# One-hot products in place of 16 gathers of the last pair but one, and the last sorts cut to 384 wide with a small write behind each operation

## The chip, the cores and the metric

The kernel runs on one core of a Trainium2 chip. The time is that of one execution of the program on the device, in microseconds (us). The engines are PE (matrix products), DVE (element-wise work on vectors), ACT (functions, scaled copies), POOL (here the issuer of all indirect transfers) and SP (the issuer of plain transfers). Each runs its own instructions in order; they wait for each other by semaphores.

## What is computed

The input is a batch of 16 graphs of 1024 nodes with 64 channels each, and an adjacency matrix of 1024 x 1024 per graph. Features are normalized, some neighbours of each node are dropped, and then each node takes, channel by channel, three quantiles of its remaining neighbours:

```python
h = jnp.maximum(_layernorm(x, axis=-1), 0.0)
...
rem = neigh & (sk > 1) & (rank % sk == sk - 1) & mask[:, :, None]
rem = rem | jnp.swapaxes(rem, 1, 2)
nd = jnp.where(rem, 0.0, adj_) > 0
s = jnp.sort(jnp.where(nd[..., None], x[:, None, :, :], jnp.inf), axis=2)
...
for tau, w in zip((0.25, 0.5, 0.75), (0.25, 0.5, 0.25)):
    agg = agg + w * (v_lo + frac * (v_hi - v_lo))
out = x + agg
y = jnp.maximum(out @ W1 + b1, 0) @ W2 + b2
```

Here `x` is the normalized `h`; the layer's result is the input plus `y`. `v_lo` and `v_hi` are the sorted neighbours at the two ranks around `tau` times the count of neighbours less one.

## The kernel before

**Stages.** The graphs go in pairs, 0 to 7. For each graph, `prepare` loads the adjacency, drops edges, orders the nodes by their count of neighbours, and writes a list of neighbour indices (`collect`, which leaves `lists[b]`). The normalized features go to a table in device memory (`gtab`). Then every node's neighbours are gathered from that table, sorted channel by channel by a network of minima and maxima, weighted, summed on PE, put back in the nodes' own order by a product with a one-hot matrix (`one_hot`, tile `at_p`, and `sums`), and sent through the two small dense layers (`mlp`).

**Tiles and classes.** After the ordering, a graph's nodes are 8 tiles of 128, the ones with most neighbours first. A tile's nodes have a fixed number of slots for neighbours; `FULL` says how many slots of each tile are gathered. `CLASSES` joins tiles with equal networks: tile 0 (13 slots), tiles 1 to 3 (11), tiles 4 and 5 (9), tiles 6 and 7 (7). The gathered values of a class and a pair lie in one tile of memory: `g0` and `g1` with two buffers, `g4` and `g6` with one, so the gathers of a pair for tiles 4 to 7 can't start before the sort of these tiles in the pair ahead is read. Nodes with very many neighbours (32 of each graph) get further slots in a sort of their own for every eight graphs, the group (`gg`, `aggregate_group`).

**Gathers.** One indirect transfer, issued by POOL, fetches one slot of one tile of one graph: 128 rows of 64 numbers (`gather` in `fetch`, L1332). A pair has 126 of them. The last pair has 70: for it the first slots of tiles 0 to 5 (`LEAST`: 8, 4, 4, 4, 4, 4, 0, 0 slots) are not gathered but computed by one-hot products, 56 in all.

**One-hot products.** `begin_pick` reads the features of the last pair's graphs back from the table (`xt`), splits each number into three parts of 16, 8 and 8 bits (`terms`) and turns the index lists to numbers (`index`). `pick` works through the wanted slots in chunks of eight: PE spreads each slot's indices over all partitions (`rowsT`, L1382), ACT copies them (`rows`, L1388), DVE compares them with the node numbers (`hot`, L1392, eight operations of 128x1024), PE multiplies (`got`, L1401, 8 products for each slot), ACT joins the parts in `g` (L1412, L1413). `hot` shares the tag "wide", of one buffer, with `rem` and `perm` of the preparation; `terms` shares "at", `index` shares "keys", both of two buffers; `xt` has one.

**Sorts.** `sort` goes through a plan of steps; a step is a minimum and a maximum over up to three pairs of slots at once (L1440, L1445, and L1437 where only one of them is wanted). Operations are at most `PART` = 384 elements wide, and each has a write of one column behind it (`opened`, the tile `pause`, L859). For the last pair and the last group (`whole`) they may be `WHOLE` = 1024 wide and have nothing behind them. From pair 5 on the weights are applied by ACT (L1460), for the group by DVE (L1462); then PE sums (L1466). In the last pair tiles 0 to 3 come first, then tiles 4 to 7 for one graph at a time.

**Order.** The loop over pairs at the end of `list_layer` only writes the program down: `weave` mixes the results of pair m - 1, the gathers and a side stream (preparation of later graphs, or `pick`). `arrange` then gives every engine an order of its own, for the whole program at once: it knows the dependences and a cost for each instruction (1345 ns for a gather), and goes forwards and backwards over the program six times with a list of ready instructions for each engine. It also ties each gather to instructions of DVE and ACT that its plan has 25 us earlier (`LEASH`). Buffers of one tag follow each other in the order in which the program names them. Small writes by `opened` follow their instruction directly.

Of the kernel before, what the change touches and what calls it, by code (L numbers as in the profile page):

```python
# [47 lines left out]
NT = N // P  # L48
# [16 lines left out]
CLASSES = (((0,), 13), ((1, 2, 3), 11), ((4, 5), 9), ((6, 7), 7))  # L65

LEAST = (8, 4, 4, 4, 4, 4, 0, 0)
# [3 lines left out]
GROUP = 8  # L71
# [481 lines left out]
ACTP, ACTB = 5, 13  # L553
# [259 lines left out]
def list_layer(  # L813
# [15 lines left out]
    B = x.shape[0]  # L829
# [463 lines left out]
    pairs = B // 2  # L1293
# [14 lines left out]
            turn[0] += 1  # L1308
            many = None if many is None else many - 1

    def opening(some, m=B // 2 - 1):

        tiles, slots = some
        if (m, tiles) not in gathered:
            gathered[m, tiles] = wk.tile(
                [P, PLANS[slots][0], len(tiles), 2, C], F32, name=f"g{tiles[0]}", bufs=2 - tiles[0] // 4
            )

    def fetch(m, classes=CLASSES, halves=(0, 1)):

        for tiles, slots in classes:
            lo, n = tiles[0], len(tiles)
            held, order = PLANS[slots][:2]

            def begin(h, tiles=tiles, lo=lo, n=n, slots=slots, held=held):
                opening((tiles, slots), m)
                nc.scalar.copy(gathered[m, tiles][:, slots - 1, :, h], owns[m][:, lo:lo + n, h])

            issued, given_out = paced

            def gather(h, slot, k, at, tiles=tiles, lo=lo):
                ins = nc.gpsimd.indirect_dma_start(  # L1332
                    out=gathered[m, tiles][:, slot, k - lo, h], out_offset=None, in_=tables[2 * m + h][0],
                    in_offset=bass.IndirectOffsetOnAxis(ap=lists[2 * m + h][:, at:at + 1], axis=0),
                    element_offset=tables[2 * m + h][1], engine_sem=issued,
                )
                given_out[ins.ins.name] = ins
                return ins

            for h in halves:  # L1340
                queue.append(partial(begin, h))
                for k in tiles:
                    for s, slot in enumerate(order[:FULL[k] + ((k, FULL[k]) in HOSTS)]):
                        if m < pairs - 1 or s >= LEAST[k]:
                            queue.append(partial(gather, h, slot, k, PASSED[k] + s))

    def begin_pick():

        first = wk.tile([P, NT], F32, name="first", bufs=1)
        nc.vector.tensor_tensor(first, own2.rearrange("p (t k) -> p t k", k=2)[:, :, 0], own2.rearrange("p (t k) -> p t k", k=2)[:, :, 1], OP.add)  # L1350
        nc.vector.tensor_scalar(first, first, float(FRONT), None, OP.add)
        terms, index = [], []
        for h in range(2):
            b = 2 * (pairs - 1) + h
            xt = wk.tile([P, NT, C], F32, name="xt", bufs=1)
            tab, at = tables[b]
            nc.sync.dma_start(
                out=xt, in_=tab[at // C + FRONT:at // C + FRONT + N].rearrange("(t p) c -> p t c", p=P)
            )
            t = wk.tile([P, NT, 3 * C], BF16, name="terms", tag="at", bufs=2)  # L1360
            halves, bytes_ = (
                xt.rearrange("p t c -> p (t c)").bitcast(d).rearrange("p (t c k) -> p t c k", t=NT, c=C)
                for d in (BF16, U8)
            )
            nc.scalar.copy(t[:, :, :C], halves[:, :, :, 1])
            nc.scalar.copy(t[:, :, C:].rearrange("p t (c k) -> p t c k", k=2), bytes_[:, :, :, 0:2])
            terms.append(t)
            f = wk.tile([P, PASSED[-1]], F32, name="index", tag="keys", bufs=2)
            nc.scalar.copy(f, lists[b])
            index.append(f)  # L1370
        return first, terms, index

    def pick(first, terms, index, wanted):

        m = pairs - 1
        for n in range(0, len(wanted), 8):
            some = wanted[n:n + 8]
            rows = wk.tile([P, len(some), P], F16, name="rows", tag="dist", bufs=2)
            for at in range(0, len(some), 4):
                tp = psum.tile([P, 4, P], F32, name="rowsT", tag="mx", bufs=3)  # L1380
                settle([
                    nc.tensor.matmul(  # L1382
                        tp[:, q], index[h][:, PASSED[k] + s:PASSED[k] + s + 1].to_broadcast([P, P]), ident32,
                        start=(q == 0), stop=(q == 3), skip_group_check=True,
                    )
                    for q, (h, k, s) in enumerate(some[at:at + 4])
                ])
                nc.scalar.copy(rows[:, at:at + 4], tp)  # L1388
            yield 0.5
            hot = wk.tile([P, NT, 8, P], BF16, name="hot", tag="wide", bufs=1)  # L1390
            for j in range(NT):
                opened(nc.vector.tensor_scalar(hot[:, j, :len(some)], rows, first[:, j:j + 1], None, OP.is_equal))  # L1392
                if j % 2:
                    yield 1.0
            for at in range(0, len(some), 2):
                (h, k, s), (h2, k2, s2) = some[at:at + 2]
                tiles, slots = next(c for c in CLASSES if k in c[0])
                to = PLANS[slots][1][s:s + 2]
                got = psum.tile([P, 2, 3 * C], F32, name="got", tag="code", bufs=2)
                settle([  # L1400
                    nc.tensor.matmul(  # L1401
                        got[:, q], hot[:, j, at + q], terms[h][:, j], start=(j == 0 and q == 0),
                        stop=(j == NT - 1 and q == 1), skip_group_check=True,
                    )
                    for q in range(2) for j in range(NT)
                ])
                opening((tiles, slots))
                step = to[1] - to[0]
                end = to[1] + (1 if step > 0 else -1)
                line = gathered[m, tiles][:, to[0]:end if end >= 0 else None:step, k - tiles[0], h]  # L1410
                halves, bytes_ = (line.bitcast(d).rearrange("p s (c k) -> p s c k", c=C) for d in (BF16, U8))
                nc.scalar.copy(halves[:, :, :, 1], got[:, :, :C])  # L1412
                nc.scalar.copy(bytes_[:, :, :, 0:2], got[:, :, C:].rearrange("p s (c k) -> p s c k", k=2))  # L1413
                yield 1.0
# [81 lines left out]
    def aggregate(m, o, between=None):  # L1496


        last = m == pairs - 1
        coef = coefs[m]  # L1500
        for half in (0, 1) if last else (1, 0):
            parts = CLASSES[2 * half:2 * half + 2][::1 if last else -1]
            for sides in ((0, 1), (1, 2)) if last and half else ((0, 2),):
                hs, one = slice(*sides), sides[0] if last and half else None
                if not one:
                    shape = [P, 4, 2, C] if one is None else [P, 2, 4, C]
                    tag, bufs = ("mx", 3) if last and not half else ("agg", 2)
                    whole = psum.tile(shape, F32, name="acc", tag=tag, bufs=bufs)
# [23 lines left out]
                for tiles, slots in parts:  # L1532
                    lo, n = tiles[0], len(tiles)
                    g = gathered[m, tiles]
                    plan = PLANS[slots]
                    if one is None:
                        lines, weigh = g.rearrange("p s n h c -> p s (n h c)"), partial(
                            lambda s, many, lo, n: coef[:, s:s + many, lo:lo + n].rearrange("p s n h -> p s (n h)"),
                            lo=lo, n=n,
                        )  # L1540
                    else:
                        lines, weigh = g[:, :, :, one], partial(
                            lambda s, many, lo, n, h: coef[:, s:s + many, lo:lo + n, h], lo=lo, n=n, h=one
                        )
                    yield from sort(
                        lines, plan, window(tiles, slots)[0], weigh, acc[:, lo - 4 * half:lo - 4 * half + n],
                        m >= ACTP, last,
                    )
                    if sides[1] == 2:
                        gathered.pop((m, tiles))  # L1550
# [143 lines left out]
    def aggregate_group(grp):  # L1694
# [9 lines left out]
        for k in range(n)[::-1]:  # L1704
            yield from sort(
                gg[:, :, k], PLANS[(CAP, SECOND + 1)[k]], window((0,), CAP)[0],
                lambda s, many: coef[:, s:s + many, k:k + 1], acc[:, k], whole=grp == B // GROUP - 1,
            )
        o = wk.tile([P, n * C], F32, name="go", tag="lows", bufs=1)
        nc.scalar.copy(o, acc.rearrange("p k c -> p (k c)"))  # L1710
# [79 lines left out]
    def drain(*gens):  # L1790
        for g in gens:
            for _ in g:
                pass
# [39 lines left out]
    for m in range(pairs + 1):  # L1833
# [15 lines left out]
            nc.vector.tensor_scalar(flag, fp, 0.0, None, OP.is_gt)  # L1849
        side = chain(*(prepare(b) for b in (2 * m + 2, 2 * m + 3) if b < B))  # L1850
        if m == pairs - 1:
            side = pick(*begin_pick(), [
                (h, k, s) for tiles, _ in CLASSES[:3] for h in range(2) for k in tiles for s in range(LEAST[k])
            ])
            for _ in range(20):
                next(side)
# [190 lines left out]
```

## Time and profile before

| | us |
|---|---|
| median of 3 runs | 1443.4 (1442.67 to 1445.76) |
| the profiled execution | 1448.98 |
| its span, first to last instruction | 1447.2 |
| busy: PE / DVE / ACT / POOL | 1100.0 / 1220.1 / 1041.4 / 1049.3 |
| DVE busy in 1350 to 1400 / 1400 to 1447 | 48.0 of 50 / 20.2 of 47 |
| gathers (L1332) from 1350 to 1400 | 27 |
| first and last hot operation (L1392) | 1155.7 and 1313.6 |

Times in the views are counted from the start of the span. A row of groups names the line, the engine, the operation and its tiles, then the count, the busy time in us and the mean ns of one, and behind the second bar the idle time of the engine just ahead of these instructions with what ended it. A row of the timeline has the start, the length, and in brackets the idle time ahead with its releaser. A row of the table by stage has the stage's limits, its length, and then the busy time and (x) the count for PE, PE's weight loads, DVE, ACT and POOL, the granted clock of PE as a share of full speed, the share of the transfer engines and GB/s. DVE's operations overlap a little: one starts before the record of the one ahead ends, so what an operation costs is the distance between starts.

### The profile page before, as it was taken

Reading aid. Unit: us, or ns where it says so; the run is one execution under the profiler, and the core shown is the slowest. Engines: PE = TensorE matmul, PEld = TensorE weight load, DVE = VectorE, ACT = ScalarE, POOL = GpSimd, SP = SyncE. Lnnn points to the kernel's source line nnn. Section 1 sums busy time; section 2 is a strip of 40 time slices with the busy share of each in tenths; the row PEclk is TensorE's granted clock in tenths of the full one; section 3 lists DMA queues with packets and bytes.
Section 4 is the critical chain, followed back from the end, with each engine's and each line's share of the span. In section 5 each row is a group of like instructions: output and inputs, shape, how many; then the busy total and the mean of one; then the engine's idle time right before and its main releaser. Section 6 shows DMA issues by size and latency. Waiting matters only on the chain. (4 is left out here: it accounts for less than half of the span.)

```text
span 1447.2 us, 30238 instructions
## 1 busy us (share of the span) xinstructions
PE 1100.0 (76%) x9011; PEld 706.0 (49%) x9011; DVE 1220.1 (84%) x5869; ACT 1041.4 (72%) x2869; POOL 1049.3 (73%) x991
## 2 busy tenths in 40 slices
PE   6877887999888985898479986599837995358167
PEld 4545555555555553555246554365514674125044
DVE  5646799978899899978799898998799779979765
ACT  8797698888959893879558773758839763449554
POOL 0277777777777777777777777777777777778880
PEclk9999998999999997899789997699969998669568
DMA  6453334333524252325332342422211111112110
GB/s 218 141 174 106 111 119 127 90 90 102 148 56 131 64 154 54 100 59 148 91 87 65 88 127 60 118 61 64 69 24 40 32 27 24 24 31 61 35 20 21
DMA packets 128831, 121.67 MB, mean 84 GB/s; under 512 B 95730, under 2 KB 96274, under 8 KB 128658
## 3 DMA queue, kind: packets, MB, share of 16 engines
q1 hardware_dynamic: 97106, 87.29, 19.9%
q0 software_dynamic: 31552, 32.36, 10.2%
q8 instruction: 73, 1.20, 0.3%
q14 instruction: 100, 0.82, 0.2%
HBM read 108.79 MB, written 9.05 MB: 81 GB/s over the span
## 5 line engine op out<-in xcount | busy, mean ns | idle before, releaser
L1332 POOL DMA_INDIRECT g<-gtab,idx x952 | 1013.1, 1064 | 354.3 <-DMA g<-gtab,idx 154.8
L1440 DVE TENSOR_TENSOR g<-g 128x384 f32<-128x384 f32 (+2 forms) x659 | 312.0, 494 | 25.3 <-DMA g<-gtab,idx 19.1
L1445 DVE TENSOR_TENSOR g<-g 128x384 f32<-128x384 f32 (+2 forms) x659 | 310.8, 493 | 5.5 <-DMA gg<-g 4.2
L1145 PE MATMUL codeP<-pack,perm 128*128 128x332 bf16 x1024 | 181.0, 318 | 54.3 <-DVE perm L1120 34.0
L1466 PE MATMUL acc<-g,kf 128*128 128x128 f32 (+2 forms) x472 | 137.6, 424 | 69.0 <-ACT g L1460 46.3
L1048 ACT ACTIVATE dist<-rk,bias 128x512 f16<-128x512 f32 x256 | 169.7, 723 | 23.8 <-DVE bias L1023 10.1
L1145 PEld LDWEIGHTS <-perm 128*128 128x128 bf16 x1024 | 94.1, 100 | 132.8 <-DVE perm L1120 48.2
L981 ACT ACTIVATE ne<-tp 128x512 fp8e4<-128x512 f32 x248 | 144.7, 640 | 12.5 <-PE tp L974 11.1
L1071 ACT ACTIVATE kept<-kp 128x512 fp8e4<-128x512 f32 x224 | 138.4, 642 | 14.3 <-PE kp L1066 5.8
L1460 ACT ACTIVATE g<-g,coef 128x64 f32<-128x64 f32 x336 | 89.2, 359 | 81.4 <-DVE g L1440 63.2
L968 PE MATMUL tp<-kb,sg 128*128 128x128 bf16 x1024 | 107.7, 232 | 47.9 <-ACT dist L1048 27.5
L961 ACT ACTIVATE sg<-at 128x1024 bf16<-128x1024 f32 x122 | 133.8, 1097 | 4.0 <-DMA at<-in_adj_dram 3.9
L1466 PEld LDWEIGHTS acc<-g,kf 128*128 128x128 f32 x472 | 81.5, 210 | 99.2 <-ACT g L1460 56.0
L1038 PE MATMUL rk<-kb,cnt 128*128 128x512 bf16 x256 | 102.2, 399 | 35.9 <-ACT dist L1048 24.1
L1043 PEld LDWEIGHTS <-ne 128*128 128x128 fp8e4 x1024 | 82.2, 101 | 86.0 <-issue 55.9
L859 DVE MEMSET pause<- 128x1 bf16 x2043 | 120.5, 59 | 0.0
L968 PEld LDWEIGHTS <-sg 128*128 128x128 bf16 x1024 | 79.9, 104 | 79.7 <-issue 57.5
L1043 PE MATMUL rk<-kw,ne 128*128 128x128 fp8e5 x1024 | 108.6, 227 | 0.0
L1158 ACT CAST st<-codeP 128x4 bf16<-128x4 f32 x128 | 21.4, 167 | 119.8 <-DVE rest L1156 88.2
L1066 PE MATMUL kp<-kw,rem 128*128 128x128 fp8e5 x1024 | 101.1, 219 | 0.0
L1061 PE MATMUL kp<-ne,kw 128*128 128x512 fp8e4 x256 | 97.5, 382 | 3.5 <-ACT dist L1048 1.4
L1062 PE MATMUL kp<-rem,kw 128*128 128x512 bf16 x256 | 97.5, 381 | 0.0
(202 smaller groups left out, 2371.6 us busy)
## 6 DMA issues: line engine op xcount, KB each, us to landing
at<-in_adj_dram SPq DMA_DIRECT2D x122, 512.0 KB
g<-gtab,idx POOLq DMA_INDIRECT x952
xt<-in_x_dram SPq DMA_DIRECT2D x16, 256.0 KB
y<-in_x_dram SPq DMA_DIRECT2D x16, 256.0 KB
gtab<-xt SPq DMA_DIRECT2D x16, 256.0 KB
out_dram<-y SPq DMA_DIRECT2D x14, 256.0 KB
spare<-in_adj_dram SPq DMA_DIRECT2D x6, 512.0 KB
gg<-g SPq DMA_DIRECT2D x32, 48.0 KB
```

Of the source, the lines that this page charges most:

```text
L859: tails[nc.vector.memset(pause[:, at:at + 1], 0.0).ins.name] = ins.ins.name
L961: nc.scalar.activation(sg, at, AF.Sign)
L968: run.append(nc.tensor.matmul(tp[:, s], sg[:, m * P:(m + 1) * P], ident16, start=(s == 0), stop=(s == 3 and t // 4 != n), skip_group_check ...
L981: nc.scalar.activation(to, tp, AF.Relu, saturate=False)
L1043: run.append(nc.tensor.matmul(rk[:, s * P:(s + 1) * P], ne[:, 4 * n + s, ts], upper, start=False, stop=(s == 3), skip_group_check=True,))
L1048: nc.scalar.activation(dist[:, n * HALF:(n + 1) * HALF], rk, AF.Abs, bias=bias[:, t:t + 1])
L1071: nc.scalar.activation(kept[:, 4 * n:4 * n + 4], kp, AF.Relu, saturate=False)
L1145: run.append(nc.tensor.matmul(flat, perm[:, t, k * P:(k + 1) * P], pack[:, t], start=False, stop=(t == NT - 1), skip_group_check=True,))
L1332: ins = nc.gpsimd.indirect_dma_start(out=gathered[m, tiles][:, slot, k - lo, h], out_offset=None, in_=tables[2 * m + h][0], in_offset=bass ...
L1440: nc.vector.tensor_tensor(at(f + k * df, df, many), pa, pb, OP.min if what == "<" else OP.max)
L1445: nc.vector.tensor_tensor(pa if back else pb, pa, pb, OP.max if what == "<" else OP.min)
L1466: nc.tensor.matmul(acc, ident32, lines[:, s], start=False, stop=(s == now[-1] and not ends), skip_group_check=True)
```

## The change

Two things. `sort` is called with `whole` false for the last pair and the last group too, so their operations are at most 384 wide and each has the write of one column behind it. And `pick`, which worked for the last pair alone, takes the pair as an argument: for the last pair but one the four first slots of tiles 4 and 5 (`CLASSES[2]`), of both graphs, 16 in all, are left out of the gathers and are one-hot products. They are written down ahead of the stream that computes the last pair's.

```diff
-    def opening(some, m=B // 2 - 1):
+    def opening(some, m):
...
-                        if m < pairs - 1 or s >= LEAST[k]:
+                        if s >= LEAST[k] or k not in picked(m):
                             queue.append(partial(gather, h, slot, k, PASSED[k] + s))
 
-    def begin_pick():
+    def picked(m):
+
+        return range(NT) if m == pairs - 1 else CLASSES[2][0] if m == pairs - 2 else ()
+
+    def first_nodes():
...
+        return first
+
+    def begin_pick(m):
+
         terms, index = [], []
         for h in range(2):
-            b = 2 * (pairs - 1) + h
+            b = 2 * m + h
...
-        return first, terms, index
-
-    def pick(first, terms, index, wanted):
-
-        m = pairs - 1
+        return terms, index
+
+    def pick(m, first, terms, index, wanted):
+
...
-                opening((tiles, slots))
+                opening((tiles, slots), m)
...
                     yield from sort(
                         lines, plan, window(tiles, slots)[0], weigh, acc[:, lo - 4 * half:lo - 4 * half + n],
-                        m >= ACTP, last,
+                        m >= ACTP, False,
                     )
...
-                lambda s, many: coef[:, s:s + many, k:k + 1], acc[:, k], whole=grp == B // GROUP - 1,
+                lambda s, many: coef[:, s:s + many, k:k + 1], acc[:, k], whole=False,
...
         if m == pairs - 1:
-            side = pick(*begin_pick(), [
+            first = first_nodes()
+            drain(pick(pairs - 2, first, *begin_pick(pairs - 2), [
+                (h, k, s) for h in range(2) for k in picked(pairs - 2) for s in range(LEAST[k])
+            ]))
+            side = pick(pairs - 1, first, *begin_pick(pairs - 1), [
                 (h, k, s) for tiles, _ in CLASSES[:3] for h in range(2) for k in tiles for s in range(LEAST[k])
             ])
             for _ in range(20):
```

`first_nodes` holds the two lines that made `first` in `begin_pick` before.

## The prediction

> **What bounds the kernel now.** I read the page first, for the busiest engines.
>
> ```profile
> PE 1100.0 (76%) x9011; PEld 706.0 (49%) x9011; DVE 1220.1 (84%) x5869; ACT 1041.4 (72%) x2869; POOL 1049.3 (73%) x991
> L1332 POOL DMA_INDIRECT g<-gtab,idx x952 | 1013.1, 1064 | 354.3 <-DMA g<-gtab,idx 154.8 <-DVE idx L1189 61.5 <-DVE pause L859 20.0
> ```
>
> POOL is called 73% busy, yet it never rests: its timeline has a gap of 0.30 us before every gather and (but for 0.83 us at 1211) no longer one from 1150 to 1412. 952 gathers of 1.06 + 0.37 us are 1367 us, nearly the span. Next the chain of waits, at its end:
>
> ```profile
> 1408.79 0.94 POOL g L1332
> 1410.04 2.64 DMA g<-gtab,idx
> 1412.90 0.76 DVE g L1440 x2
> ```
>
> The last gathers release the last sort on DVE, and from its last merge (1427) some 14 us of PE, ACT and DVE lead to 1441. What DVE waited for between 1211 (where the merges of pair 6's tiles 1 to 3 begin) and 1441, first by releaser and then in the timeline:
>
> ```profile
> DVE g L1440 <- DMA g<-gtab,idx: 19.1, 4, 8.6
> DVE g L1531 <- ACT g L1528: 11.7, 3, 9.0
> DVE highs L1615 <- ACT highs L1614: 6.5, 2, 5.7
> ```
>
> ```profile
> 1349.45 1.01 DVE L1440 TENSOR_TENSOR g<-g 128x768 f32<-128x768 f32 x1 [8.62 <-DMA g<-gtab,idx]
> 1410.63 0.11 DVE L1531 MEMSET g<- 32x64 f32 x1 [9.02 <-ACT g L1528]
> 1412.90 0.76 DVE L1440 TENSOR_TENSOR g<-g 128x256 f32<-128x256 f32 x2 [2.16 <-DMA g<-gtab,idx]
> ```
>
> The 9.02 us stand under ACT, but that ACT copy (L1528) itself waited 9.47 us for a gather: it is the same wait. So gathers cost DVE time at the end, but DVE has little to give beyond it, as the stages show:
>
> ```profile
> 1211.00:1286.00 75.00, 18.93 (x88) 11.42 (x88) 63.66 (x303) 26.04 (x103) 58.06 (x54) 0.63 0.13 26
> 1286.00:1350.00 64.00, 49.90 (x284) 30.65 (x282) 53.37 (x207) 53.48 (x110) 52.12 (x40) 0.93 0.23 54
> 1350.00:1403.00 53.00, 23.88 (x91) 16.44 (x91) 49.51 (x117) 26.32 (x87) 44.16 (x30) 0.61 0.09 18
> 1403.00:1441.00 38.00, 27.14 (x142) 15.25 (x142) 18.70 (x55) 16.76 (x51) 8.95 (x10) 0.87 0.09 19
> ```
>
> The third busy column is DVE: 185.2 of 230 us. Of the 44.8 idle, 9.3 lie in the closing 14 us; 35.5 are open to be won.
>
> **Part one: 16 gathers go.** Two tiles (4, 5), four slots, two batches. They stand among the 48 gathers of pair 6's tiles 4 to 7. From the gather at 1217.51 to that at 1264.78 there are 33 steps in 47.27 us: 1.43 us each, so POOL is 16 x 1.43 = 22.9 us earlier from there on. It issues no others in their place.
>
> **What it adds for them:** two more chunks of eight products (now seven, L1392 and L1401).
> - DVE: 16 hot operations, started 0.41 us apart = 6.6 us.
> - PE: 128 products and 16 transposes; chunks follow each other in 9.0 to 9.3 us while the clock is 1.00 (hots at 1184.2, 1193.6, 1202.7), so 18.4 us. PE was busy 47 of 50 us in 1150 to 1200 but 23 of 50 in 1200 to 1250, so they push later chunks into free time.
> - ACT: 4 rows (0.58), 8 pairs of copies into g (0.30 + 0.38), two terms (0.62 + 1.06) and two index copies (0.27): 11.7 us, in 1150 to 1200, where it had 20 us idle. SP: two loads of 256 KB from gtab, behind which the two of the last pair queue (xt has one buffer, terms and index two). The first load of pair 7 was ready by 1093, 62 us ahead of the first hot, which is its cover. Uncovered, it would be some 7 us of PE.
>
> The new chunks need the buffer "wide" after perm of batch 15, so they start where pair 7's first did, at 1155.7, and the second needs a key buffer of batch 15, ready at 1164; pair 7's chunks move back two places. Its products for tiles 1 to 3 are needed from 1245, the first merge of 768, at the earliest, and would be there by 1230, so that has cover; the 6.6 us of DVE land in 1211 to 1244, where DVE had none, and count in full. If they fit before 1211 (14 us idle in 1150 to 1211) they cost nothing: that is the other end.
>
> **Part two: the last sorts.** Three things change at L1440, L1445, L1437, L1462 for pair 7 and the last group.
> - Width: only tiles 1 to 3 were wider than 384 (32 operations of 128x768, 30 of them after 1286). One takes 0.87 us from start to start, two of 384 with a pause 2 x 0.48 = 0.96: +0.09 x 32 = 2.9 us; L1437 was narrower.
> - The pause: merges of 256 start every 0.345 us with it (1261.17 to 1263.94) and every 0.335 without (1390.1 to 1394.8); some 270 operations x 0.012 = 3.2 us.
> - Gathers beside them. They are slow only beside merges without the pause:
>
> ```profile
> L1332 POOL DMA_INDIRECT g<-gtab,idx x727 | 757.1, 1041 | 224.7 <-DMA g<-gtab,idx 108.8 <-DVE pause L859 17.5 <-DVE g L1445 9.4
> L1332 POOL DMA_INDIRECT g<-gtab,idx x8 | 20.8, 2598 | 2.4 <-DMA g<-gtab,idx 1.2 <-DVE gg L1445 0.6 <-ACT g L1413 0.3
> ```
>
> ```profile
> 1317.51 3.48 POOL L1332 DMA_INDIRECT g<-gtab,idx  x1 [0.30 <-DVE y L1663]
> 1323.25 4.88 POOL L1332 DMA_INDIRECT g<-gtab,idx  x1 [0.30 <-DMA g<-gtab,idx]
> 1372.01 8.20 POOL L1332 DMA_INDIRECT g<-gtab,idx  x1 [0.30 <-DVE gg L1440]
> ```
>
> The first line is 200 to 1200, with pauses, the second 1317 to 1339, without, when DVE ran gg merges end to end. At 1.08 us each (as beside paused merges in 1253 to 1264) the 8 gathers there give back 12.2 us and the 28 of 1350 to 1403 (42.5 us) 12.3: 24.5 us more.
>
> The Trainium skill speaks against this: "SBUF — State Buffer", Who interferes with whom, holds (as an inference) that a two-input tensor_tensor takes only the read side of the port it shares with GpSimd, while writing descriptors needs the write side. By that the pauses free nothing and the 24.5 us stay. The rows above contradict it for trains without a gap; by the page the last gather would land at 1391 and not at 1367, and the sum below would hardly move, since DVE could get to it at 1390 at the earliest.
>
> **The sum.** The last gather, issued at 1411.3, comes at 1411.3 - 22.9 - 24.5 = 1364: gathers no longer set the end, DVE does. From 1211: 35.5 us of idle go, 6.6 + 2.9 + 3.2 = 12.7 come: 22.8 us at best. What is late next: waits that no gather causes stay (gg on the copies of set_apart 2.0, flag on PE 1.6), and after tiles 1 to 3 are merged (1381.6 now, then about 1372) PE has 44.4 us and ACT 35.0 us of work which stood in 59 us and would have 47: PE would be 94% busy, in order, and I take 5 us lost there, an estimate with ends 0 and 10. In all 8.6. So 22.8 - 8.6 = 14.2, less 1 for two hand-overs between hot and PE of about 0.5 (1.46 and 0.19 us shown): **13.2 us**. The profiled execution took 1448.98 us (span 1447.2); its span would be 1434. It lies 5.6 us above the median 1443.4, a constant I carry over: **1430 us**.
>
> **Rivals.**
> 1. *DVE was the bound already.* Only waits that end on a gather by name go: 19.1 - 12.7 = 6.4 us, so 1437, between 1434 and 1443. For it: 49.5 of 53 us busy in 1350 to 1403. Against: the 9.02 us above are a gather's too.
> 2. *Everything packs.* The chunks' hots fall into idle time ahead of 1211, nothing is lost at PE: 35.5 - 2.9 - 3.2 = 29.4, so 1414; with the hots paid in full 22.8, so 1421. For it: the order of every engine is worked out anew for the whole program, and gathers that keep their pace hold better to a plan that gives all of them one cost. Against: PE's 94%.
> 3. *Slower: the hot buffer.* "wide" is one buffer, and DVE runs in order: a hot operation that stands in its queue before PE has finished the chunk ahead holds up every merge behind it, and the class weights on ACT and the sums on PE wait for those. Four chunks would lie past 1211, two more than now, where the clock is 0.63 on the mean against 1.00. If each takes there what the first one takes now (1155.75 to 1175.17, 19.4 us, though that one waited for an index list) in place of 9.2, DVE stands 4 x 10.2 = 41 us: 1443.4 - 22 + 41 = 1462. It decides from a chunk of 9.2 + 22/4 = 14.7 us. Against: chunks two to five kept 9.2 us, and hots can be spread between merges, as those of 1220 to 1243 were.
>
> **How the numbers follow.** The forecast has 0.50 (1422 to 1440), rival 1 has 0.20, rival 2 0.12, rival 3 0.18. This kernel's measurement can tell about 0.2% (2.9 us) from no change: 0.05 of rival 1 and 0.02 of rival 3 lie within it. Faster 0.50 + 0.15 + 0.12 = 0.77, same 0.07, slower 0.16. Range 1417 to 1446: half-way between rival 2's ends, and up to where rival 3 begins.
>
> **What would show it.** Right: 936 gathers, none above 2 us after 1300, the last issued near 1364; DVE over 90% busy from 1211 to its last merge, near 1405, with no wait over 3 us on a gather; nine chunks of hots. Wrong: DVE waits for PE at hots, above 14 us a chunk (rival 3); DVE idle as before under other names (rival 1); gathers still of 3 to 8 us (then the pauses free nothing). The time itself would be wrong if POOL's pace ahead of 1211 shifted with the new order, where I take it as unchanged: 1% of it is 11 us.

## The result, and the profile after

| | before | changed |
|---|---|---|
| median of 13 runs each, us | 1443.4 (1437.30 to 1447.63) | 1436.33 (1430.43 to 1440.32) |
| the profiled execution | 1448.98 | 1437.93 |
| its span | 1447.2 | 1436.2 |

The ratio of the times is 0.9952, with an interval of 0.9938 to 0.9966: the changed kernel is faster by 7.1 us, or 0.48%; the forecast of 1430 us had meant 13.4. The two profiled executions differ by more, 11.0 us of span, and that difference turned out to be the main lesson of this case.

The page of the changed kernel and its row of gathers:

```profile
PE 1120.9 (78%) x9171; PEld 721.4 (50%) x9171; DVE 1233.6 (86%) x6277; ACT 1052.2 (73%) x2895; POOL 1016.4 (71%) x975
L1332 POOL DMA_INDIRECT g<-gtab,idx x936 | 978.7, 1046 | 351.3 <-DMA g<-gtab,idx 153.8 <-DVE idx L1189 62.7 <-DVE pause L859 16.1
```

There are 16 gathers fewer and 160 PE instructions more (128 products, and 32 that spread indices, where the prediction counted 16), and DVE is busy 13.5 us longer. The end of POOL's work, from its timeline:

```profile
1375.12 0.94 POOL L1332 DMA_INDIRECT g<-gtab,idx  x1 [0.30 <-DMA g<-gtab,idx]
1381.87 1.09 POOL L1759 DMA_INDIRECT out_dram<-gx,gto  x1 [5.80 <-DVE g L1532]
```

The last gather now starts 36 us earlier than in the profile before (1411.29), and after it POOL waits for DVE instead of DVE for POOL. What DVE waited for in the last stage, 1190 to 1436 (lines of the changed kernel: L1669 is the place of L1662 before, L1622 of L1615, L1399 of L1392):

```profile
DVE yp L1669 <- PE yp L1665: 9.1, 5, 3.4
DVE highs L1622 <- ACT highs L1621: 7.1, 2, 6.2
DVE hot L1399 <- ACT g L1420: 3.1, 1, 3.1
DVE highs L1622 <- PE low L1601: 1.4, 1, 1.4
DVE g L1538 <- ACT g L1535: 0.5, 1, 0.5
```

No line ends on a gather any more; 28.1 us did before (19.1 by name and the 9.0 of L1531, which an ACT copy passed on). The table by stage, with DVE as the third busy column:

```profile
1211.00:1286.00 75.00, 37.86 (x267) 29.04 (x265) 74.61 (x379) 33.21 (x133) 58.26 (x55) 0.70 0.20 41
1286.00:1350.00 64.00, 50.51 (x274) 29.87 (x271) 60.69 (x369) 54.32 (x114) 51.49 (x42) 0.89 0.19 39
1350.00:1403.00 53.00, 27.19 (x96) 18.90 (x97) 48.94 (x283) 31.54 (x101) 22.90 (x19) 0.60 0.07 12
1211.00:1414.80 203.80, 127.36 (x698) 84.00 (x696) 194.60 (x1090) 125.43 (x365) 132.65 (x115) 0.75 0.15 31
```

From 1211 to its last merge at 1414.8 (1426.9 before) DVE is busy 194.6 of 203.8 us, 95%. The largest hole left in this stretch is

```profile
1375.35 0.30 DVE L1669 TENSOR_TENSOR yp<-yp,gapart 128x128 f32<-128x128 f32 x1 [3.35 <-PE yp L1665]
```

In the chain of waits the piece ahead of it is 7.53 us of sums on PE (`gacc`, L1473), then ACT and the dense layers of the few nodes: DVE waits in order for a result of PE that came late.

DVE doesn't set the end to the very last, though. In the chain of waits of the changed kernel its merges stand up to 1397.6, and then

```profile
1397.16 0.41 DVE g L1447
1397.59 1.31 ACT g L1467 x5
1398.94 5.49 PE acc L1473 x24
```

From 1398.94 to 1427.9 the chain is PE's alone, but for 0.38 us of ACT: PE works off its queue in order (27.4 of 28.8 us busy from 1400 on), and DVE's last merges, which end at 1414.8, are not on it. Before, DVE was on it up to 1422.3.

One gather did not behave as the others:

```profile
1341.28 12.67 POOL L1332 DMA_INDIRECT g<-gtab,idx  x1 [0.30 <-ACT at_p L1574]
```

All others after 1200 take at most 1.31 us. Before, seven took 2.1 to 8.2 us, 29.9 us in all. The 12.67 us stand beside merges that do have the write behind them, which the prediction had not allowed for.

### The profile page after: what moved, and what is told of

It reads as the page before. It is cut to its first block, busy times and chain, and to the rows that moved or that the text cites. A ratio compares the mean times of both kernels' runs of the same rounds, so it can differ in the third digit from the quotient of the medians.

```text
span 1436.2 us, 30966 instructions
## 1 busy us (share of the span) xinstructions
PE 1120.9 (78%) x9171; PEld 721.4 (50%) x9171; DVE 1233.6 (86%) x6277; ACT 1052.2 (73%) x2895; POOL 1016.4 (71%) x975
## 3 DMA queue, kind: packets, MB, share of 16 engines
q8 instruction: 74, 1.21, 0.4%
## 4 chain that ended last, share of the span: by engine, by line
ACT 28%; issue 25%; PE 17%; DVE 16%; DMA 2%; POOL 1%; DVEq 0%; SPq 0%; POOLq 0%; ACTq 0%
ACT kept L1071 4%; PE codeP L1145 4%; DVE g L1447 4%; ACT dist L1048 4%; DVE g L1452 4%; ACT ne L981 2%; ACT sg L961 2%; PE acc L1473 2%; ACT waste L1243 2%; ACT g L1467 2%; ACT waste L1238 2%; PE high L1595 1%; PE got L1408 1%; PE low L1601 1%; DMA g<-gtab,idx 1%
## 5 line engine op out<-in xcount | busy, mean ns | idle before, releaser
L1332 POOL DMA_INDIRECT g<-gtab,idx x936 | 978.7, 1046 | 351.3 <-DMA g<-gtab,idx 153.8
L1447 DVE TENSOR_TENSOR g<-g 128x384 f32<-128x384 f32 (+2 forms) x675 | 312.8, 483 | 1.0 <-issue 0.2
L1473 PE MATMUL acc<-g,kf 128*128 128x128 f32 (+2 forms) x472 | 136.7, 424 | 38.5 <-ACT g L1467 20.0
L859 DVE MEMSET pause<- 128x1 bf16 x2403 | 141.8, 59 | 0.0
L1038 PE MATMUL rk<-kb,cnt 128*128 128x512 bf16 x256 | 101.2, 395 | 36.0 <-ACT dist L1048 26.2
L1473 PEld LDWEIGHTS acc<-g,kf 128*128 128x128 f32 x472 | 83.5, 216 | 66.0 <-ACT g L1467 27.4
```

The source lines that it names most:

```text
L859: tails[nc.vector.memset(pause[:, at:at + 1], 0.0).ins.name] = ins.ins.name
L1332: ins = nc.gpsimd.indirect_dma_start(out=gathered[m, tiles][:, slot, k - lo, h], out_offset=None, in_=tables[2 * m + h][0], in_offset=bass ...
L1447: nc.vector.tensor_tensor(at(f + k * df, df, many), pa, pb, OP.min if what == "<" else OP.max)
L1473: nc.tensor.matmul(acc, ident32, lines[:, s], start=False, stop=(s == now[-1] and not ends), skip_group_check=True)
```

## The experiments

Three theories stood against each other. A: each part alone takes the wait for POOL away, and then DVE sets the end, so either part gives most of the gain. B: the parts add up, about half each. C: only the products gain, and the writes cost what they free.

One thing has to be known to read what follows. The experiments are six sets of runs, and in five of them every kernel, the one before too, took some 1837 us in place of 1443. It isn't a matter of the chip alone: one and the same chip took 1444 us in one set and 1831 in a later one. The ratios below are always to the kernel before in the same set, but they tell little of the 7 us, since the kernels timed beside it there hardly waited for gathers. The lengths of single gathers could be read all the same.

**The kernel before once more.** No edit; one run, in the one set with undisturbed times (some 1443 us).

> The kernel before once more, for its profile. Theory: the long gathers come from the order of the program, not from chance, so they stand at the same merges with about the same lengths: seven over 2 us in the last stage (3.5, 4.9, 2.2, 5.1, 8.2, 2.1, 3.8 in the profile of before), and a DVE wait on a gather near the end. Rival: they are chance, and their number and lengths differ by half or more. On a chip that takes about 1443 us for this kernel the span should be some 4 us under the first profile's 1447.2, near the median of the runs.

It took 1444.14 us, with a span of 1442.3. What DVE waited for in 1190 to 1436, and the long gathers:

```profile
DVE g L1440 <- DMA g<-gtab,idx: 11.7, 4, 5.5
DVE g L1531 <- ACT g L1528: 7.8, 3, 5.3
DVE highs L1615 <- ACT highs L1614: 6.5, 2, 5.7
DVE yp L1662 <- PE yp L1658: 4.5, 3, 2.4
```

```profile
1327.28 4.27 POOL L1332 DMA_INDIRECT g<-gtab,idx  x1 [0.30 <-DVE gg L1445]
1331.85 2.24 POOL L1332 DMA_INDIRECT g<-gtab,idx  x1 [0.30 <-DMA g<-gtab,idx]
1335.87 5.14 POOL L1332 DMA_INDIRECT g<-gtab,idx  x1 [0.30 <-DMA g<-gtab,idx]
1372.38 6.47 POOL L1332 DMA_INDIRECT g<-gtab,idx  x1 [0.30 <-DMA g<-gtab,idx]
1396.04 2.42 POOL L1332 DMA_INDIRECT g<-gtab,idx  x1 [0.30 <-DMA g<-gtab,idx]
```

Five long ones, 20.5 us, where the first profile has seven and 29.9. Two lengths come back to the hundredth (2.24 and 5.14) and the stretches are the same, 1317 to 1342 and 1372 to 1402; the rest differ. So the order of the program seems to set where gathers grow long, and the execution how many and how long: neither theory alone. The last gather starts at 1405.92, 5.4 us earlier than in the first profile, and the span is 4.9 us shorter. That is nearly all of the 5.6 us by which the first profiled execution lay above the median.

With it the balance of DVE from 1211 can be made against two executions of the kernel before:

| | first profile before | before once more | changed |
|---|---|---|---|
| last gather starts | 1411.29 | 1405.92 | 1375.12 |
| DVE's last operation ends | 1440.7 | 1435.3 | 1428.8 |
| DVE busy from 1211 to there | 185.2 | 186.4 | 198.8 |
| DVE idle from 1211 to there | 44.5 | 37.9 | 19.0 |

Against the first profile the change wins 25.5 us of idle time and pays 13.6 us of work: 11.9. Against the second it wins 18.9 and pays 12.4: 6.5, close to the difference of the medians, 7.1.

**The changed kernel again, and each part alone.** The products alone:

```diff
-                        m >= ACTP, False,
+                        m >= ACTP, last,
...
-                lambda s, many: coef[:, s:s + many, k:k + 1], acc[:, k], whole=False,
+                lambda s, many: coef[:, s:s + many, k:k + 1], acc[:, k], whole=grp == B // GROUP - 1,
```

The shorter operations and the writes alone, in the kernel before (called "writes alone" below, though the width is in it too):

```diff
-                        m >= ACTP, last,
+                        m >= ACTP, False,
...
-                lambda s, many: coef[:, s:s + many, k:k + 1], acc[:, k], whole=grp == B // GROUP - 1,
+                lambda s, many: coef[:, s:s + many, k:k + 1], acc[:, k], whole=False,
```

And the changed kernel with the products for one of the two tiles only, eight in place of sixteen:

```diff
-        return range(NT) if m == pairs - 1 else CLASSES[2][0] if m == pairs - 2 else ()
+        return range(NT) if m == pairs - 1 else CLASSES[2][0][:1] if m == pairs - 2 else ()
```

Expected of the changed kernel again, the products alone, the writes alone and the eight products, in the first set:

> The changed kernel once more, as the reference for the other runs of this call. Expected 1436 us, 7 us under the kernel before. Its profile tells whether the one gather of 12.7 us at 1341 belongs to the order of the program (then it is there again, at the same gather) or falls where it likes.

> The 16 products without the shorter operations and the writes behind them. Theory A (both parts take away the same wait, after which DVE sets the end): DVE has 6.6 us more than in the kernel before and not 13.6, the last gather is issued near 1388 and DVE gets to the last sort near 1385, so 1436 plus or minus 3 us. Rival B (the parts add up): about half of the gain, 1440. Rival C (only the products gain and the writes are paid for): 1436 - 6 = 1430.

> The shorter operations and the writes behind them without the 16 products. Theory A: no gather above 2 us after 1300 in most executions, last gather issued 24 us earlier, near 1387; DVE pays 6.1 us and still waits some 6.7 us for pair 6's gathers, so 1437 plus or minus 3. Rival B: 1440. Rival C: the writes free nothing, 1443 + 6 = 1449.

> As the changed kernel, but the products of tile 4 alone: 8 gathers go and one chunk comes. Theory A (DVE sets the end): DVE has 3.3 us less, the gathers end 11 us later and are still ahead of DVE, so 1433. Rival B (gathers still count): 8 gathers of 1.4 us back, 1436 + 5 or more = 1441.

And in the later sets:

> The products alone again, since the first run of it was on a chip on which every engine stood still for 2.5 to 3 us every 8 us or so and everything took 1.28 times as long. Theory A (both parts take away the same wait, then DVE sets the end): ratio 0.995, as for the whole change, plus or minus 0.002. Rival B (the parts add up): 0.9975. Rival C (the products gain, the writes are paid for): 0.991.

> The shorter operations and the writes alone, again. Theory A: 0.996 plus or minus 0.002, gathers after 1300 near 1.1 us each, the last issued near 1387. Rival B: 0.9975. Rival C: 1.004.

> The kernel before with only the shorter operations and the writes behind them at the end. If the chip runs the kernel before at about 1443 us: theory A (both parts take away the same wait) 1436 to 1439 us, no DVE wait on a gather after 1350 us and one long gather at most; theory B (half each) 1439 to 1441; theory C (only the products gain, the writes are paid for) 1443 to 1447, later than before by the 3 to 6 us that the writes and the narrower operations cost. If the kernel before takes some 1837 us again, within 0.3% of it, and only the lengths of the gathers count: one over 10 us, the rest under 2.

> The products alone, beside a kernel before of about 1444 us and a changed kernel of 1436. Theory A (either part takes the wait for POOL away, then VectorE sets the end): 22.9 us of gathers gone bring the last gather from 1411 to about 1388 us, VectorE has 6.1 us less to do than in the changed kernel (no writes, no narrower merges): 1430 to 1436 us, the long gathers stay (five to seven over 2 us) and no VectorE wait on a gather after 1350 us. Theory B (each part gives half): 1440 us, with waits on gathers left. Theory C (only the products gain): 1430 us.

> The shorter operations and the writes alone, same comparison. Theory A: POOL gets 24.5 us of long gathers back, the last gather comes at about 1387 us, VectorE has 6.1 us more than before and 6.6 us less than in the changed kernel: 1430 to 1437 us, one long gather at most, no VectorE wait on a gather after 1350 us. Theory B: 1440 us. Theory C (the writes cost what they free): 1444 to 1447 us.

> The changed kernel with eight of its sixteen new products (one of the two tiles of each slot). If VectorE sets the end (theory A), eight hots less at 0.41 us give 3.3 us: 1433 us, 3 us faster than the changed kernel, with the last gather some 11 us later and still not waited for. If POOL still has a part in it, 1438 to 1442 us and a VectorE wait on a gather at the end.

> The shorter operations and the writes alone, once more, for a chip that takes about 1444 us for the kernel before (the changed kernel: 1436). Theory A (either part takes the wait for POOL away, then VectorE sets the end): 1430 to 1437 us, one long gather at most, no VectorE wait on a gather after 1350 us. Theory B (each part gives half): 1440 us. Theory C (the writes cost what they free, only the products gain): 1444 to 1447 us. On a chip that takes some 1837 us for both, within 0.3% of the kernel before, and only the lengths of the gathers count.

Measured, ratio to the kernel before of the same set (1830.8 to 1837.3 us) with its interval, and the gathers of 2 us or more in the profile:

| kernel | ratio | long gathers: number, sum in us |
|---|---|---|
| changed, again | 1.0047 (1.0021 to 1.0074) | 1, 13.43 |
| products alone, first | 1.0032 (1.0000 to 1.0065) | 7, 47.8 |
| second | 0.9997 (0.9970 to 1.0023) | 5, 33.7 |
| third | 1.0042 (1.0012 to 1.0073) | 7, 47.8 |
| writes alone, first | 1.0045 (1.0012 to 1.0078) | 1, 17.16 |
| second | 1.0014 (0.9987 to 1.0041) | 1, 17.15 |
| third | 1.0014 (0.9984 to 1.0044) | 1, 17.15 |
| fourth | 1.0027 (0.9995 to 1.0060) | 0 |
| fifth | 1.0030 (1.0006 to 1.0055) | 1, 17.15 |
| eight products | 1.0026 (1.0002 to 1.0050) | 0 |
| again | 1.0004 (0.9980 to 1.0028) | 0 |

What POOL waited for, in the changed kernel of the first of these sets:

```profile
L1332 POOL DMA_INDIRECT g<-gtab,idx x936 | 967.6, 1034 | 760.9 <-issue 287.9 <-DMA g<-gtab,idx 76.2 <-DVE idx L1189 61.6
```

The gathers themselves take 967.6 us, no more than the 978.7 of the undisturbed profile; but POOL is idle 760.9 us ahead of them, not 351.3, and 287.9 of it end on nothing that the profile shows. DVE, ACT and PE have gaps of 2 to 3 us of the same sort, most of them at other moments than POOL's. (An expectation above says that every engine stood still; in the timelines all four are seldom idle together.) DVE's list of waits in the last stage names a gather in one of these eleven profiles, for 1.0 us. So there was hardly anything to be gained there by freeing POOL, as far as these versions tell (the kernel before has no profile in that condition), and the changed kernel is 0.47% slower.

*What follows for the long gathers.* The products alone leave five to seven of them, in all three profiles; wherever the narrower operations and the writes are in, there is one or none, in all nine profiles that have them (the first of the changed kernel among them). So part two does it, not the products. Of its two halves the width can't be the cause for most: of the seven long gathers of the first profile before, six stand beside operations of at most 384 wide, which the change left as wide as they were, and only the one of 8.20 us beside 128x768. What differs there is the write, and the order of the engines, which each edit changes too; that the order has no share wasn't tested. Two rows of POOL's timeline with the products alone (the third profile), and two with the writes alone (the fifth):

```profile
1721.52 11.75 POOL L1332 DMA_INDIRECT g<-gtab,idx  x1 [0.30 <-DMA g<-gtab,idx]
1735.50 18.39 POOL L1332 DMA_INDIRECT g<-gtab,idx  x1 [0.30 <-DMA g<-gtab,idx]
```

```profile
1744.05 17.15 POOL L1332 DMA_INDIRECT g<-gtab,idx  x1 [0.30 <-DMA g<-gtab,idx]
1761.50 1.21 POOL L1332 DMA_INDIRECT g<-gtab,idx  x1 [0.30 <-DMA g<-gtab,idx]
```

The one that is left even with the writes is no accident of one execution: it comes back in four of five profiles of the writes alone, three times at 17.15 us. DVE runs this beside its first part:

```profile
1744.05 0.54 DVE L1445 TENSOR_TENSOR g<-g 128x384 f32<-128x384 f32 x1
1744.07 0.06 DVE L859 MEMSET pause<- 128x1 bf16 x1
1744.53 0.34 DVE L1445 TENSOR_TENSOR gg<-gg 128x192 f32<-128x192 f32 x1
1744.55 0.06 DVE L859 MEMSET pause<- 128x1 bf16 x1
```

Merges of the pair's `g` and of the group's `gg` alternate without a gap, each with its write. The 12.67 us gather of the changed kernel stands beside the same mixture. But the very next gather, beside more of it, takes 1.21 us (1.07 in the changed kernel).

Where such a gather ends belongs to DVE's program and not to the gather. In the changed kernel it is the 17th gather from the end the first time (1341.28 to 1353.95) and the 8th the second time (1750.61 to 1764.04), and each ends 1.02 to 1.03 us after the start of the same merge:

```profile
1352.92 0.21 DVE L1444 TENSOR_TENSOR gg<-gg 128x64 f32<-128x64 f32 x1
1750.61 13.43 POOL L1332 DMA_INDIRECT g<-gtab,idx  x1 [0.30 <-DMA g<-gtab,idx]
1763.02 0.21 DVE L1444 TENSOR_TENSOR gg<-gg 128x64 f32<-128x64 f32 x1
```

The same holds in all nine profiles with a gather above 12 us, the four of the writes alone and the three of the products alone (18.39 to 18.41 us) among them: it ends 1.02 to 1.04 us after the start of a 128x64 merge of the group, the only one of that width that starts beside it. Yet in the three profiles with the writes and without a long gather those beside the same merges take 0.94 to 1.34 us. Why one gather is held and another is not stays open, and so does what lets it go.

*What follows for the time.* How the 7.1 us divide between the two parts stays open too. A, B and C give forecasts for a kernel that takes 1443 us, and the parts alone were never seen in that condition. The ratios do fit one half of the account, what the edits cost where nothing is gained: the plain means are 1.0026 for the writes alone (4.8 us of 1834) and 1.0024 for the products alone (4.4 us), together 9.2, and both together cost 1.0047, 8.6 us. The prediction had 6.1, 6.6 and 12.7 us of DVE work for these. The eight products don't fit (2.8 us on the mean, where 9.4 would be due), and every interval is some 0.3% wide, so this is consistent and not shown.

**Not run.** More products (tiles 1 to 3 of the last pair but one as well), which would have raised DVE's bill by 9.8 us (24 hots of 0.41 us), and the width apart from the writes. No version but the kernel before and the changed one has a time from an undisturbed set.

## Why the prediction was right, and where its sizes were off

1. **16 gathers and 22.9 us of POOL: right.** 936 gathers are left, and none took the place of those. The last gather of pair 6 starts 24.4 us earlier (1246.60 for 1271.02), of which 1.3 us were there ahead of the 16 (gather 844 at 1214.74 for 1216.07).
2. **The writes give POOL back its pace: right but for one gather.** Of 29.9 us of long gathers 12.67 are left. The prediction had put the last gather at 1364; it starts at 1375.12, and those 11 us are about the 12.67 less the usual 1.1 to 1.3. The statement that gathers "are slow only beside merges without the pause" falls: six of the nine profiles with the writes, of two programs, show one of 12.67 to 17.16 us beside merges that have them. It cost DVE nothing here: no wait of its ends on a gather.
3. **The page that spoke against it.** By the inference in the Trainium skill, "SBUF — State Buffer", Who interferes with whom, the writes should have freed nothing and the last gather landed at 1391, that is been issued at 1411.3 - 22.9 = 1388.4. The measurement decides against it for these gathers: the last was issued at 1375.12 though 12.67 us of a long one were left, and five to seven long ones stand against one or none when only part two differs. Which port or wait holds a gather no run here shows.
4. **DVE takes over as the bound: right up to 1397.6.** 95% busy to the last merge, no wait on a gather; behind 1397.6 PE's queue sets the end. Rival 1 (DVE was bound already, 1437) names a time close to the median, but not by its reason: it had the waits come back under other names and only 6.4 us go, and 28.1 us of waits on gathers went, with a gain in span of 11.0.
5. **DVE's new work 12.7: measured 13.6** against the first profile, 12.4 against the second.
6. **Idle time won, 35.5 less 8.6 less 1, so 25.9: measured 25.5, in part by luck.** The 5 us of congestion came behind the same engine: from 1211 to the last merge DVE waits 6.6 us for `yp` on PE, where it waited nothing (1.9 in the second profile of before), and 1.4 for `low`; the group's sums of 7.53 us stand ahead of the largest of these waits. But the 2.0 and 1.6 us that were to stay are gone, so the sum fits better than its terms. Tiles 1 to 3 were merged at 1380.4, not at "about 1372". The time given for the last merge, "near 1405", wasn't consistent with this sum, which gives 1426.9 - 13.2 = 1413.7; it is 1414.8.
7. **The sum of 13.2: the span fell by 11.0.** DVE's end came 11.9 us earlier; the last stores then took 7.4 us where they had taken 6.5.
8. **"A constant I carry over", 5.6 us: this step failed**, as far as two executions can tell, and it is the larger part of the 6.3 us by which 1430 missed 1436.33. The 5.6 us by which the profiled execution lay above the median were no fixed offset. The second profile of before, 0.7 us above the median, shows what they were: longer gathers, 29.9 us in the first against 20.5, and with them a last gather 5.4 us later. That is the very wait which the change removes, so most of it could be won only in that execution. The changed kernel's own profile lies 1.6 us above its median, 1437.93 - 1436.33. With 1.6 in place of 5.6 the same sum gives 1434.2, and the other 2.2 us are its own error in the span (13.2 for 11.0, point 7).
9. **Rival 3 (the hot buffer) didn't come.** Hots were pushed behind 1211, as foreseen, and from 1223.5 to 1290.1 there are 30 of them, 17.8 us for eight, above the 14.7 us from which this rival should have decided. But merges ran between them, and behind 1211 no hot waited: the pace of the chunks was the wrong sign to watch, the wait ahead of a hot the right one. Ahead of 1211 hots did wait, 3.26 and 4.77 us for PE and 3.14 for ACT, 11.2 us where it had been 3.5; the "two hand-overs of about 0.5" were too few. It cost DVE little, since other waits there were shorter: 48.4 us busy in 1150 to 1211 for 49.4. **Rival 2** (everything packs) needed the hots ahead of 1211; they ran on to 1290. (DVE had 11.6 us idle from 1150 to 1211, 61 less 49.4, not the 14 of the prediction.)

## What to carry to other kernels

A profile is one execution. Where its time lies above the median of the runs, ask first which wait makes it longer, with a second profile of the same program if one can be had. If it is the wait that the change takes away, the gain against the median is smaller by that much. And when a wait is removed whose engine was only just behind another, cost the change by the next engine's idle time and new work: here 25.5 us won and 13.6 paid gave the 11.9 us by which that engine's end moved, while the last gather moved by 36, more than DVE could use.

## What the runs showed of the hardware

- The time in which POOL issues one gather depends on what DVE runs beside it: in the last stage mostly 0.94 to 1.34 us beside merges with a write of one column behind each, up to 18.41 us beside merges without. The writes don't always help: one gather of 12.67 to 17.16 us was left in two programs (six of nine profiles) beside alternating merges, and the next one was short.
- A gather above 12 us ended 1.02 to 1.04 us after the start of one and the same 128x64 merge of its program, in all nine profiles that have one, whichever gather it was. The cause isn't known.
- Two executions of the same program differed by 4.9 us of span (1447.2 and 1442.3), with seven long gathers of 29.9 us and five of 20.5 us; the last gather came 5.4 us earlier in the second, though POOL had been 1.4 us later at 1318.
- In five sets of runs all kernels took 1.27 times as long, with gaps of 2 to 3 us on every engine, many of which end on nothing in the profile (287.9 us of idle time ahead of POOL's gathers). Single operations of POOL and DVE kept their length (gathers 1034 ns on the mean against 1046; merges of L1447 486 against 483 ns), while PE's took longer at a lower granted clock (L1038 448 against 395 ns, 0.833 against 0.908). A cause isn't known; it came and went on one chip.
